# Two pairs of experts per visit, an earlier first block of weights, and stores by halves in a fused GRU and mixture-of-experts kernel

## The chip, the cores and the metric

The kernel runs on one core of a Trainium2 chip. The metric is the device time of one execution in microseconds; for the kernel before it is 2645.92 us, the median of three runs (2645.7 to 2645.97). A core has a matrix engine (TensorE, PE in the profile), three engines for elementwise work (VectorE or DVE, ScalarE or ACT, GpSimd or POOL) and a queue engine (SyncE or SP). DMAs are issued here from SP and POOL. Each engine works through its own list of instructions in order, and semaphores tie the lists together.

## The reference

Two blocks follow each other on x of shape (128, 64, 512), float32: 128 batch rows, 64 time steps, 512 channels. Cut to what matters:

```python
# block 0: a GRU over time, its states through a ternary-weight matrix, added to x
x = x + ffn0(gru(cond, x, W_ih, W_hh, b_ih, b_hh), weight, bias)
# block 1: a causal convolution over 64 steps, and on it a mixture of experts
h = causal_conv(x, taps=cond[:, None, :]) + b
logits = h @ gate_w.T                       # 64 experts, the best 6 of each token
for each token t, each of its experts e (at most 64 tokens per expert):
    y[t] += p[t, e] * (silu(h[t] @ w_gate[e]) * (h[t] @ w_up[e])) @ w_down[e]
shared = silu(h @ sw_gate) * (h @ sw_up) @ sw_down
out = x + y + shared
```

The sizes are H = 512 channels, I = 352 inner channels for an expert and 704 for the shared one; w_gate, w_up and w_down hold 64 experts.

## The kernel before, in words

**The GRU stage** (to about 1400 us in the profile) runs its 64 steps; it is not touched. It leaves x after block 0 in DRAM, in `out` and, by channels, in `x1c`.

**The convolution stage** (1400 to 1466 us) goes through 16 slabs of 32 channels, each against a Toeplitz matrix built from cond (`conv_group`, L182). Buffers `tz0` to `tz3` and `xc0` to `xc3` serve the slabs in turn. L713 adds the bias and writes the result to `hids`, one tile for the first 32 time steps and one for the last 32; L725 adds the products with the two oldest taps, held in `xl`. A time step t has 128 batch rows. `store_first` writes the first four time steps to the table `tab` in DRAM from POOL; the experts later gather their rows there. The last slab's 32 channels of these rows are copied to a tile of their own, `copy`, and stored from it.

**Turning and routing.** `turn` transposes a time step's rows on PE (L1108), and L1118 copies the turned rows back over the same place in `hid`, which must wait until the stores out of that place have landed. `route` makes the logits (`lg`, L1132), the softmax and the six best experts. NB = 4 time steps make an iteration i; there are NI = 16.

**The shared expert** (`shared(i)`) is a generator with 44 pieces per iteration (`PIECES`), and the order in which it is advanced is the order of PE's work. It multiplies in a Winograd form (Strassen's seven products, `winograd`, L809) on blocks of 128 inner channels; `prepare_shared(c)` makes the sums of weights for block c on DVE (`st1`, `st2`, `st4`), and overwrites part of the weights. The weights `swg` and `swu` come by one DMA each, after the gate weights `gw` and the remainder `swr`. In the last iteration the results are added to what stands in `out` (`sums`), and the rows are stored whole from SP (L1079). The earlier iterations add their rows to `out` by accumulating DMAs from POOL (`add_shared`, L1086).

**The experts.** After iteration 8, pairs of experts are woven into the pieces of `shared`. Two experts of 64 slots each share the 128 rows of a pair, each on 64 columns of PE. A pair q goes through four steps: `inputs` transposes the gathered rows (L1478), `gate_up` makes the two products (`pg`, `pu`, L1498) and the gated values `a`, `turn` transposes `a` (L1513), `down` multiplies by w_down (`py`, L1524), copies to `ys` (L1533) and scatters with accumulation to `out` from POOL (L1535). `experts()` is a generator of EPIECES = 97 pieces, which the main loop spreads over the pieces of `shared`:

```python
            while due < EPIECES and due * PIECES * SPREAD < slot * 4 * EPIECES:
                next(routed)
                due += 1
```

So between two pieces of the experts lie two or three of the shared expert. Four sets of buffers (`wexs`) hold the weights of two pairs, loaded from SP by `load_gate_up` and `load_down` as soon as PE has read what they replace. The rows of iterations 8 to 15 wait in DRAM (`xts`) and are loaded by `load_xrows` into two buffers in turn (L1271), on the same SP queue. The gathers (L1455) and scatters stand on POOL's queue. The tile framework gives the order on each engine from the order of the program and an estimate of its own; `tc.issue_after` puts an instruction behind a named one.

Of the kernel before, what the change touches and what calls it, by code (L numbers as in the profile page):

```python
# [8 lines left out]
F32 = mybir.dt.float32  # L9
# [10 lines left out]
P = 128  # L20
B = 128
T = 64
D = 512
# [9 lines left out]
DS = 16  # L33
# [9 lines left out]
def adaln_ffn_kernel(  # L43
# [641 lines left out]
        nc.vector.tensor_add(xl[:, 1], xl[:, 1], tap[:, 1])  # L685


    copy = conv.enter_context(tc.tile_pool(name="copy", bufs=1)).tile([P, 4, 2 * DS], F32, name="copy")

    def store_first(d, rows=None):  # L690
        for t in range(4):
# [5 lines left out]
    with tc.tile_pool(name="ps_c", bufs=4, space=PSUM) as ps_c:  # L697
        for sl in range(NSL):

            if sl >= NCB:  # L700
                load_piece(sl)
            if sl == NSL - 1:

                store_first(slice(0, 2 * DS * (NSL - 2)))
                store_first(slice(2 * DS * (NSL - 2), 2 * DS * (NSL - 1)))
            for g in range(DS // 4):
                if early:
                    ps = early.pop(0)
                else:
                    ps = conv_group(sl, g, ps_c.tile([P, D], F32, name="psc"))  # L710
                d = slice(g * 4, g * 4 + 4)
                for th in range(2):
                    nc.vector.tensor_tensor(  # L713
                        hids[th][:, :, 2 * DS * sl : 2 * DS * (sl + 1)].rearrange(
                            "p t (h d) -> p t h d", h=2
                        )[:, :, :, d],
                        ps[:, :, :, th * TH : (th + 1) * TH].rearrange("p j h t -> p t h j"),
                        cb_h[:, sl, :, d].unsqueeze(1).to_broadcast([P, TH, 2, 4]),
                        ALU.add,
                    )  # L720
            if sl >= NCB:
                if sl == NCB:
                    tail_products()
                d = slice(0 if sl == NCB else 2 * DS * sl, 2 * DS * (sl + 1))
                nc.vector.tensor_add(  # L725
                    hids[1][:, TH - TAIL :, d], hids[1][:, TH - TAIL :, d], xl[:, :, d]
                )
            if sl == NSL - 1:
                nc.scalar.copy(copy, hids[0][:, :4, D - 2 * DS :])
                store_first(slice(D - 2 * DS, D), copy)  # L730
    conv.close()
    gis_.close()

# [15 lines left out]
    st4 = w1.tile([P, HK, full * P], F32, name="st4")  # L749
    st2 = w1.tile([P, HK, full * P], F32, name="st2")  # L750
    st1 = w1.tile([P, HK, full * P], F32, name="st1")
    gw = w1.tile([P, KD, NE], F32, name="gw")
    load_rows(gw, gateT)

    swr = w1.tile([P, KD, 2, rest], F32, name="swr")
    load_rows(swr[:, :, 0, :], sw_gate[:, full * P :])
    load_rows(swr[:, :, 1, :], sw_up[:, full * P :])
    swg = w1.tile([P, KD, full * P], F32, name="swg")
    load_rows(swg, sw_gate[:, : full * P])
    swu = w1.tile([P, KD, full * P], F32, name="swu")  # L760
    loaded = load_rows(swu, sw_up[:, : full * P])

    swdr = w1.tile([P, D], F32, name="swdr")

    sws = {1: swg[:, :HK], 2: swg[:, HK:], 3: swu[:, HK:], 4: st4, 5: st1, 6: st2, 7: swu[:, :HK]}

    def prepare_shared(c):

        w11, w12, w21, w22, t4, t1, t2 = (
            w[:, :, c * P : (c + 1) * P]  # L770
            for w in (sws[1], sws[7], sws[2], sws[3], st4, st1, st2)
        )
        nc.vector.tensor_sub(t1, w12, w11)
# [48 lines left out]
    class Block:  # L822
# [5 lines left out]
        def product(self, n):  # L828
            ps = winograd(
                n,  # L830
                self.accs,
                lambda k: sws[n][:, k, self.c * P : (self.c + 1) * P],
                lambda k: self.ops[n][:, k],
            )
            one, two = self.aT[:, :QT], self.aT[:, QT:]
            if n == 1:
                self.u2 = shu.tile([P, QT], F32, name="u2")
                nc.scalar.copy(self.u2, ps)
            elif n == 6:
                add(self.u2, self.u2, ps)  # L840
            elif n == 7:
                self.u3 = sh.tile([P, QT], F32, name="u3")
                self.summed = add(self.u3, ps, self.u2)
            elif n == 5:
                add(two, ps, self.u3)
                mul(two, two, self.g2)
            elif n == 2:
                self.g1 = sh.tile([P, QT], F32, name="g1")
                nc.scalar.activation(self.g1, ps, AF.Silu)
            elif n == 4:  # L850
                self.g2 = sh.tile([P, QT], F32, name="g2")
                add(self.g2, ps, self.u2)
                nc.scalar.activation(self.g2, self.g2, AF.Silu)
            elif n == 3:
                add(one, ps, self.u2)
                mul(one, one, self.g1)
# [20 lines left out]
    class Down:  # L877
# [54 lines left out]
        def finish(self, rows, sums):  # L932
# [12 lines left out]
            for name, more in (("x", None), ("v", self.v), ("z", self.u2), ("w", self.u2)):  # L945
                j, half_ = self.places[name]
                cols = slice(half_ * HD, (half_ + 1) * HD)
                dst = rows[:, 2 * self.p + j, cols]
                if sums is not None:
                    old = sums[:, 2 * self.p + j, cols]  # L950
                    if more is not None:
                        add(old, old, more)
                    add(old, self.accs[name], old)
                elif more is None:
                    nc.scalar.copy(dst, self.accs[name])
                else:
                    add(dst, self.accs[name], more)
# [9 lines left out]
    def shared(i, sums=None):  # L967
# [44 lines left out]
        for c in range(full):  # L1012
            cur = Block(c, ops, aT)
            for n in (1, 6, 7, 3, 2, 4, 5):
# [6 lines left out]
                if n == 7 and c == 0:  # L1021

                    with tc.issue_after(cur.summed.ins):
                        rest_values()
                if n == 7 and i == 0 and c + 1 < full:
                    prepare_shared(c + 1)
            prev = cur
        if i >= PLAIN:
            after = Down(0, aT, aTr, space)
# [27 lines left out]
        else:  # L1057
            for p in range(2):
# [15 lines left out]
                for name in ("x", "w", "z"):  # L1074
                    down.block(name)
                down.finish(rows_of(i), sums)
                if sums is not None:
                    for t in range(i * NB + 2 * p, i * NB + 2 * p + 2):
                        nc.sync.dma_start(out=out_t[t], in_=sums[:, t % NB])  # L1079
                yield  # L1080
# [175 lines left out]


    slots = ctx.enter_context(tc.tile_pool(name="slots", bufs=1, reuse_waits="tile"))
    xrp = []

    def row_buffer(side):
        xrp.append(
# [4 lines left out]

    def load_xrows(i):
        if i < NI:
            xrows[i] = xrp[i % 2].tile([P, NB, D], F32, name="xr")  # L1270
            nc.sync.dma_start(  # L1271
                out=xrows[i], in_=xts[i * NB - TH : (i + 1) * NB - TH].rearrange("t p d -> p t d")
            )

    row_buffer("left")
    load_xrows(NI // 2)
# [17 lines left out]
    def load_gate_up(q):  # L1294

        if q < NE // 2:
            for e in (2 * q, 2 * q + 1):
                wg = wexs[e % 4].tile([P, KD, EI], F32, name="wg")
                load_rows(wg, w_gate[e])
                wu = wexs[e % 4].tile([P, KD, EI], F32, name="wu")  # L1300
                load_rows(wu, w_up[e])
                weights[e] = [wg, wu]

    def load_down(q):
        if q < NE // 2:
            for e in (2 * q, 2 * q + 1):
                wd = wexs[e % 4].tile([P, len(ech), D], F32, name="wd")
                load_rows(wd[:, :efull, :], w_down[e, : efull * P, :])
                nc.sync.dma_start(out=wd[:n_last, efull, :], in_=w_down[e, efull * P :, :])
                weights[e].append(wd)  # L1310

    weights = {}
    for q in range(2):
# [152 lines left out]
    class Pair:  # L1466
# [5 lines left out]
        def inputs(self):  # L1472
            q = self.q
            rows = gathered.pop(q)
            self.ws = [weights.pop(2 * q + j) for j in range(2)]
# [13 lines left out]
        def gate_up(self):  # L1489
# [5 lines left out]
            for which, acc in ((0, pg), (1, pu)):  # L1495
                for k in range(KD):
                    for j in range(2):
# [4 lines left out]
                            start=(k == 0),  # L1502
                            stop=(k == KD - 1),
                        )
            self.a = a = ex.tile([P, EI], F32, name="a")
# [12 lines left out]
        def down(self):  # L1518
# [50 lines left out]
    for i in range(NI // 2 + 1, NI):  # L1569
        n = i - NI // 2 - 1  # L1570
        sums = None
        if i == NI - 1:

            sums = xrp[(i + 1) % 2].tile([P, NB, D], F32, name="xr")
# [60 lines left out]
```

## Time and profile before

| | us |
|---|---|
| median of three runs | 2645.92 |
| the profiled execution | 2645.99 |
| its span, first to last instruction | 2644.3 |
| PE busy | 2632.3 |
| DVE busy | 1405.0 |
| ACT busy, POOL busy | 427.4, 453.0 |
| convolution stage | about 1400 to 1466 |
| first L1498, last L1524 | 2013.6, 2564.9 |
| last matmul's end | 2639.6 |

The granted clock of TensorE was 1.000 of full speed over the span. Busy times of different engines overlap, so only the longest chain counts. A row such as "PE y L809 <- DVE u L843" says that PE's work on tile y, line 809, waited for DVE's work on u. PE's matmuls are pipelined: the listed length of one is longer than the step to the next, so starts are compared with starts.

### The profile page before, as it was taken

What the parts mean: (1) busy time and instruction counts of PE and PEld (TensorE: products, weight loads), DVE (VectorE), ACT (ScalarE), POOL (GpSimd) and SP (SyncE); (2) the same over time, 40 slices, a digit from 0 to 9 for tenths busy, and PEclk for the clock granted to TensorE, in tenths of its full rate; (3) what the DMA queues carried; (4) which work ended last, traced back from release to release, by engine and by line L of the source; (5) the groups of instructions that cost most, each with busy time, mean ns of one, the idle gap of its engine ahead of it and who ended that gap; (6) DMA issues with size and microseconds to landing.
All of it is one profiled execution on the core that took longest, in us unless ns stands there. A gap on an engine that the chain in (4) does not pass through costs nothing.

```text
span 2644.3 us, 31163 instructions
## 1 busy us (share of the span) xinstructions
PE 2632.3 (100%) x11993; PEld 1825.1 (69%) x11993; DVE 1405.0 (53%) x3110; ACT 427.4 (16%) x794; POOL 453.0 (17%) x516
## 2 busy tenths in 40 slices
PE   9999999999999999999999999999999999999999
PEld 7666666666666666666668767788886666666667
DVE  6555555555555555555557755566674433433344
ACT  1111111111111111111110222222321111111111
POOL 2112111111111111111114100000002222222210
PEclk9999999999999999999999999999999999999999
DMA  5333233232322222322228911222356899998962
GB/s 197 75 58 66 56 60 60 54 61 53 61 47 52 44 52 44 76 44 52 44 58 297 334 37 28 39 66 64 85 145 188 281 315 285 293 332 260 295 182 48
DMA packets 476277, 323.34 MB, mean 122 GB/s; under 512 B 329056, under 2 KB 396512, under 8 KB 473952
## 3 DMA queue, kind: packets, MB, share of 16 engines
q1 hardware_dynamic: 447536, 248.18, 33.6%
q0 software_dynamic: 28592, 73.16, 11.5%
q8 instruction: 95, 1.56, 0.2%
q14 instruction: 54, 0.44, 0.0%
HBM read 235.01 MB, written 92.55 MB: 124 GB/s over the span
## 4 chain that ended last, share of the span: by engine, by line
PE 99%; DVE 0%; DMA 0%; issue 0%; ACT 0%; DVEq 0%
PE psgh L598 25%; PE psz L809 7%; PE psw L809 7%; PE psx L809 7%; PE psz L399 6%; PE psw L399 6%; PE psx L399 6%; PE psf L494 4%; PE y L809 4%; PE py L1524 3%; PE psy L399 3%; PE pg L1498 3%; PE pu L1498 3%; PE y L984 2%; PE psc L182 2%; PE lg L1132 1%
## 5 line engine op out<-in xcount | busy, mean ns | idle before, releaser
L598 PE MATMUL psgh<-whh,hT 128*128 128x512 f32 x1528 | 671.0, 595 | 0.5 <-ACT hT L471 0.5
L598 PEld LDWEIGHTS psgh<-whh,hT 128*128 128x128 f32 x1528 | 285.2, 190 | 348.5 <-issue 334.6
L399 PE MATMUL psx<-wih,xp 128*128 128x256 f32 x744 | 191.0, 379 | 0.0
L220 POOL DMA_DIRECT2D xn<-in_x_dram x61 | 33.9, 555 | 842.2 <-DVE x L506 829.6
L399 PEld LDWEIGHTS psx<-wih,xp 128*128 128x128 f32 x744 | 139.0, 190 | 18.0 <-issue 0.5
L1507 DVE SCALAR_TENSOR_TENSOR a<-a,rw,pu 128x352 f32<-128x352 f32 x32 | 18.6, 580 | 220.4 <-PE pu L1498 220.4
L625 DVE TENSOR_TENSOR n<-psgh,bhn 128x512 f32<-128x512 f32 (+1 forms) x65 | 44.3, 683 | 171.3 <-PE psgh L598 171.3
L471 ACT COPY hT<-psf 128x512 f32<-128x512 f32 x63 | 36.9, 586 | 556.7 <-PE psf L463 556.7
L609 DVE TENSOR_TENSOR r<-psgh,gi 128x512 f32<-128x512 f32 x64 | 44.3, 692 | 139.3 <-PE psgh L598 139.3
L1086 POOL DMA_DIRECT2D out_dram<-hid x32 | 27.6, 1000 | 450.6 <-issue 332.9
L490 POOL TENSOR_TENSOR xn<-xn,fb 128x512 f32<-128x512 f32 x61 | 77.1, 1263 | 143.8 <-DMA xn<-in_x_dram 143.8
L399 PE MATMUL psz<-wih,xs 128*128 128x256 f32 x372 | 95.6, 379 | 0.1
L399 PE MATMUL psy<-t,xs 128*128 128x256 f32 x372 | 95.5, 379 | 0.0
L399 PE MATMUL psw<-t,xp 128*128 128x256 f32 x372 | 95.5, 379 | 0.0
L399 PE MATMUL psz<-t,xs 128*128 128x256 f32 x372 | 95.5, 379 | 0.0
L399 PE MATMUL psw<-wih,xp 128*128 128x256 f32 x372 | 95.4, 379 | 0.0
L494 PE MATMUL psf<-sgn,hhi 128*128 128x512 f32 x256 | 95.0, 492 | 0.3 <-DVE hlo L479 0.3
L1524 PE MATMUL py<-wd,aeT 128*64 128x512 f32 (+1 forms) x384 | 89.5, 601 | 0.0
L628 ACT ACTIVATE n<-n 128x512 f32<-128x512 f32 (+1 forms) x65 | 40.4, 623 | 276.8 <-DVE n L627 276.8
L414 DVE TENSOR_TENSOR p<-psx,bi 128x512 f32<-128x512 f32 x93 | 64.3, 691 | 37.2 <-PE psx L399 37.2
L809 PE MATMUL psx<-xr,swg 128*128 128x256 f32 x320 | 83.3, 383 | 0.0
L809 PE MATMUL psx<-hid,swg 128*128 128x256 f32 x320 | 82.4, 380 | 0.0
(332 smaller groups left out, 4757.4 us busy)
## 6 DMA issues: line engine op xcount, KB each, us to landing
wg<-in_w_gate_dram SPq DMA_DIRECT2D x64, 704.0 KB
wu<-in_w_up_dram SPq DMA_DIRECT2D x64, 704.0 KB
wd<-in_w_down_dram SPq DMA_DIRECT2D x64, 512.0 KB
x1c<-x SPq DMA_DIRECT2D x62, 256.0 KB
out_dram<-x SPq DMA_DIRECT2D x62, 256.0 KB
xn<-in_x_dram POOLq DMA_DIRECT2D x61, 256.0 KB, 4.1
xp<-in_xT_dram POOLq DMA_DIRECT2D x30, 512.0 KB, 5.6
xc<-x1c SPq DMA_DIRECT2D x28, 512.0 KB
```

The source lines that it names most:

```text
L182: i = nc.tensor.matmul(ps[rows, j].rearrange("p h (u t) -> p h u t", u=2), xcs[sl % NCB][:, rows, g * 4 + j], tzs[sl % NCB][:, :, :, g * 4 ...
L399: i = nc.tensor.matmul(ps, self.ops[n][:, k, :], self.ws[n][:, k, :], start=(first and k == 0), stop=(k == HK - 1), skip_group_check=not f ...
L414: add(self.p1, both, b)
L490: nc.gpsimd.tensor_add(xn, xn, fb)
L494: nc.tensor.matmul(ps, piece[:, k, :], sgn[:, k, :], start=(i == 0 and k == 0), stop=(i == 1 and k == KD - 1),)
L598: nc.tensor.matmul(ps[:, piece], hT[:, k, :], whh[c][:, k, piece], start=(k == 0), stop=(k == KD - 1),)
L609: i = nc.vector.tensor_add(r, ps_r, gis.pop((t, 0)))
L625: nc.vector.tensor_add(n[:, p], ps_n[:, p], bhn[:, p])
L809: i = nc.tensor.matmul(ps.rearrange("p (j b) -> p j b", b=P) if len(r.shape) == 3 else ps, lhs(k), r, start=(first and k == 0), stop=(k == ...
L984: nc.tensor.matmul(gu.rearrange("p (j b) -> p j b", b=P), swr[:, k].rearrange("p w n -> p (w n)"), rows[:, k], start=(k == 0), stop=(k == ...
L1498: nc.tensor.matmul(acc[halves[j]], self.xeT[:, k, halves[j]], self.ws[j][which][:, k, :], start=(k == 0), stop=(k == KD - 1),)
L1524: nc.tensor.matmul(py[halves[j]], self.aeT[:n, c, halves[j]], self.ws[j][2][:n, c, :], start=(c == 0), stop=(c == len(ech) - 1),)
```

## The change

Five things are edited. `experts()` handles two pairs in one visit: down, gate_up, down, gate_up follow each other in one piece, and there are 81 pieces instead of 97; `load_gate_up` stands in `gate_up` instead of `turn`, and `ys` has a pool of four buffers instead of two. The rows of iterations 9 to 15 have a third buffer, and their load stands behind the newest load of w_up on SP's queue. The shared expert's weights are split: the first block of 128 inner channels of each has its own tile and is loaded ahead of the other four, and `prepare_shared` of the next block stands behind L843 of this one in iteration 0. The first four time steps' last 64 channels (two slabs instead of one) are copied to a part of `xl` that has been read, and stored from there. And in the last iteration the second two time steps are stored by halves of 256 channels, each right after its sum.

```diff
-    copy = conv.enter_context(tc.tile_pool(name="copy", bufs=1)).tile([P, 4, 2 * DS], F32, name="copy")
+    copy = xl[:, 0, : 16 * DS].rearrange("p (t d) -> p t d", t=4)
...
             if sl == NSL - 1:
-                store_first(slice(0, 2 * DS * (NSL - 2)))
-                store_first(slice(2 * DS * (NSL - 2), 2 * DS * (NSL - 1)))
+                store_first(slice(0, D - 4 * DS))
...
-            if sl == NSL - 1:
-                nc.scalar.copy(copy, hids[0][:, :4, D - 2 * DS :])
-                store_first(slice(D - 2 * DS, D), copy)
+            for n in range(2):
+                if sl == NSL - 2 + n:
+                    d = slice(2 * DS * sl, 2 * DS * (sl + 1))
+                    nc.scalar.copy(copy[:, :, n * 2 * DS : (n + 1) * 2 * DS], hids[0][:, :4, d])
+        store_first(slice(D - 4 * DS, D), copy)
...
+    swg, swu = [None, None], [None, None]
+    others = slice(P, full * P)
+    for which, sw in enumerate((swg, swu)):
+        sw[1] = w1.tile([P, KD, (full - 1) * P], F32, name=f"sw{which}")
     gw = w1.tile([P, KD, NE], F32, name="gw")
...
-    swg = w1.tile([P, KD, full * P], F32, name="swg")
-    load_rows(swg, sw_gate[:, : full * P])
-    swu = w1.tile([P, KD, full * P], F32, name="swu")
-    loaded = load_rows(swu, sw_up[:, : full * P])
+    for which, sw, src in ((0, swg, sw_gate), (1, swu, sw_up)):
+        sw[0] = w1.tile([P, KD, P], F32, name=f"sw{which}first")
+        load_rows(sw[0], src[:, :P])
+    for sw, src in ((swg, sw_gate), (swu, sw_up)):
+        loaded = load_rows(sw[1], src[:, others])
...
-    sws = {1: swg[:, :HK], 2: swg[:, HK:], 3: swu[:, HK:], 4: st4, 5: st1, 6: st2, 7: swu[:, :HK]}
+    sums_ = {4: st4, 5: st1, 6: st2}
+    blocks = {1: (swg, 0), 2: (swg, 1), 3: (swu, 1), 7: (swu, 0)}
+
+    def weights_of(n, c):
+        if n in sums_:
+            return sums_[n][:, :, c * P : (c + 1) * P]
+        sw, h_ = blocks[n]
+        at = max(c - 1, 0) * P
+        return sw[min(c, 1)][:, h_ * HK : (h_ + 1) * HK, at : at + P]
...
                     add(old, self.accs[name], old)
+                    if self.p == 1:
+                        nc.sync.dma_start(out=out_t[(NI - 1) * NB + 2 + j, :, cols], in_=old)
...
+                if n == 7 and i == 0 and c == 0:
+                    marks.append(cur.summed)
                 if n == 7 and i == 0 and c + 1 < full:
-                    prepare_shared(c + 1)
+                    with tc.issue_after(cur.summed.ins):
+                        prepare_shared(c + 1)
...
-                if sums is not None:
+                if sums is not None and p == 0:
                     for t in range(i * NB + 2 * p, i * NB + 2 * p + 2):
                         nc.sync.dma_start(out=out_t[t], in_=sums[:, t % NB])
...
-            xrows[i] = xrp[i % 2].tile([P, NB, D], F32, name="xr")
-            nc.sync.dma_start(
+            xrows[i] = xrp[(i - NI // 2) % 3].tile([P, NB, D], F32, name="xr")
+            with behind(queued):
+                nc.sync.dma_start(
...
-                load_rows(wu, w_up[e])
+                queued.append(load_rows(wu, w_up[e]))
...
     add_shared(NI // 2)
+    row_buffer("left")
     load_xrows(NI // 2 + 2)
...
+    ysp = ctx.enter_context(tc.tile_pool(name="ys", bufs=4, reuse_waits="tile"))
...
# in Pair.gate_up, after the matmuls:
+            load_gate_up(self.q + 2)
# in Pair.turn:
-            load_gate_up(self.q + 2)
# in Pair.down:
-            ys = ex.tile([P, D], F32, name="ys")
+            ys = ysp.tile([P, D], F32, name="ys")
...
-    EPIECES = 3 * NPAIR + 1
+    EPIECES = 5 * NPAIR // 2 + 1
 
     def experts():
         pairs = [Pair(q) for q in range(NPAIR)]
-        pairs[0].inputs()
+        for pair in pairs[:2]:
+            pair.inputs()
+            yield
+        for pair in pairs[:2]:
+            pair.gate_up()
         yield
-        pairs[0].gate_up()
-        yield
-        for q, pair in enumerate(pairs):
-            pair.turn()
-            yield
-            if q + 1 < NPAIR:
-                pairs[q + 1].inputs()
+        for q in range(0, NPAIR, 2):
+            for pair in pairs[q : q + 2]:
+                pair.turn()
                 yield
-            pair.down()
-            if q + 1 < NPAIR:
-                pairs[q + 1].gate_up()
+            for pair in pairs[q + 2 : q + 4]:
+                pair.inputs()
+                yield
+            for pair in pairs[q : q + 2]:
+                pair.down()
+                if pair.q + 2 < NPAIR:
+                    pairs[pair.q + 2].gate_up()
             yield
```

`weights[e]` becomes a dictionary of the three weights of expert e; its uses follow, and `sums` takes its buffer by the new count.

More of the change, by code (lines that the diff above doesn't have):

```diff
@@ L757, in adaln_ffn_kernel @@
     load_rows(swr[:, :, 1, :], sw_up[:, full * P :])
-    swg = w1.tile([P, KD, full * P], F32, name="swg")
-    load_rows(swg, sw_gate[:, : full * P])
-    swu = w1.tile([P, KD, full * P], F32, name="swu")
-    loaded = load_rows(swu, sw_up[:, : full * P])
-    swdr = w1.tile([P, D], F32, name="swdr")
-    sws = {1: swg[:, :HK], 2: swg[:, HK:], 3: swu[:, HK:], 4: st4, 5: st1, 6: st2, 7: swu[:, :HK]}
+    for which, sw, src in ((0, swg, sw_gate), (1, swu, sw_up)):
[3 more added lines that the diff above has]
+        loaded = load_rows(sw[1], src[:, others])
+    swdr = w1.tile([P, D], F32, name="swdr")
+    sums_ = {4: st4, 5: st1, 6: st2}
[6 more added lines that the diff above has]
+        return sw[min(c, 1)][:, h_ * HK : (h_ + 1) * HK, at : at + P]
     def prepare_shared(c):
[L769 to L772, printed above, removed]
+        w11, w12, w21, w22, t4, t1, t2 = (weights_of(n, c) for n in (1, 7, 2, 3, 4, 5, 6))
         nc.vector.tensor_sub(t1, w12, w11)
@@ L831, in product @@
                 self.accs,
-                lambda k: sws[n][:, k, self.c * P : (self.c + 1) * P],
+                lambda k: weights_of(n, self.c)[:, k],
                 lambda k: self.ops[n][:, k],
@@ L1258, in adaln_ffn_kernel @@
     slots = ctx.enter_context(tc.tile_pool(name="slots", bufs=1, reuse_waits="tile"))
-    xrp = []
+    xrp, queued = [], []
     def row_buffer(side):
@@ L1269, in load_xrows @@
         if i < NI:
-            xrows[i] = xrp[i % 2].tile([P, NB, D], F32, name="xr")
-            nc.sync.dma_start(
-                out=xrows[i], in_=xts[i * NB - TH : (i + 1) * NB - TH].rearrange("t p d -> p t d")
-            )
+            xrows[i] = xrp[(i - NI // 2) % 3].tile([P, NB, D], F32, name="xr")
+            with behind(queued):
+                nc.sync.dma_start(
+                    out=xrows[i],
+                    in_=xts[i * NB - TH : (i + 1) * NB - TH].rearrange("t p d -> p t d"),
+                )
     row_buffer("left")
@@ L1300, in load_gate_up @@
                 wu = wexs[e % 4].tile([P, KD, EI], F32, name="wu")
-                load_rows(wu, w_up[e])
-                weights[e] = [wg, wu]
+                queued.append(load_rows(wu, w_up[e]))
+                weights.setdefault(e, {}).update({0: wg, 1: wu})
     def load_down(q):
@@ L1309, in load_down @@
                 nc.sync.dma_start(out=wd[:n_last, efull, :], in_=w_down[e, efull * P :, :])
-                weights[e].append(wd)
+                weights.setdefault(e, {})[2] = wd
     weights = {}
@@ L1474, in inputs @@
             rows = gathered.pop(q)
-            self.ws = [weights.pop(2 * q + j) for j in range(2)]
+            self.ws = [weights[2 * q + j] for j in range(2)]
             ps = ps_e.tile([P, D], F32, name="py").rearrange("p (k b) -> p k b", k=KD)
@@ L1504, in gate_up @@
                         )
+            load_gate_up(q + 2)
             self.a = a = ex.tile([P, EI], F32, name="a")
@@ L1572, in adaln_ffn_kernel @@
         if i == NI - 1:
-            sums = xrp[(i + 1) % 2].tile([P, NB, D], F32, name="xr")
+            sums = xrp[(i + 1 - NI // 2) % 3].tile([P, NB, D], F32, name="xr")
             nc.sync.dma_start(
```

## The prediction

> **What bounds the kernel now.** I read the busy rows and the chain of the page first. TensorE (PE) is the whole span, on the single chain that ended last:
>
> ```profile
> PE 2632.3 (100%) x11993; PEld 1825.1 (69%) x11993; DVE 1405.0 (53%) x3110; ACT 427.4 (16%) x794; POOL 453.0 (17%) x516
> ...
> PE 99%; DVE 0%; DMA 0%; issue 0%; ACT 0%; DVEq 0%
> ```
>
> So only two things can pay: PE's idle time (span 2644.3 less 2632.3 busy, 12.0 us), and time in which PE counts as busy without working at its rate. The windows of ten microseconds put it at 1.1 us at the start, 0.5 before 1400, 5.7 between 1400 and 1500, and 4.7 after the last matmul. The list of who waited for whom names what this change can touch (PE of 1460 to 1500, DVE of 1464 to 1480, SP of 1800 to 2600; microseconds in all, times, the longest):
>
> ```profile
> PE pst L1108 <- DVE hid L1118: 1.3, 1, 1.3
> PE pst L1108 <- DVE hid L713: 1.0, 1, 1.0
> PE psw L809 <- DVE u L843: 0.8, 1, 0.8
> ```
> ```profile
> DVE hid L1118 <- DMA tab<-hid: 2.4, 1, 2.4
> DVE st L773 <- DMA swu<-in_sw_up_dram: 2.0, 1, 2.0
> ```
> ```profile
> SPq L101 <- PE py L1524: 167.0, 25, 15.9
> SPq L1271 <- DMA out_dram<-xr: 135.0, 9, 43.3
> ```
>
> Behind the 1.3 us stands a DMA: L1118 writes the turned rows back over hid, and the stores of hid's channels 448 to 479, issued at 1462.63, landed only at 1468.80. In the expert stage (2013 to 2565) no PE wait is listed. The other kind of loss shows in the timeline of PE across one visit to the experts (start, length, instruction):
>
> ```profile
> 2219.73 1.03 PE L809 MATMUL y<-es,st 128*128 128x256 f32 x4
> 2220.68 2.80 PE L1524 MATMUL py<-wd,aeT 128*64 128x512 f32 x12
> 2223.31 2.54 PE L1498 MATMUL pg<-wg,xeT 128*64 128x352 f32 x16
> 2225.68 2.54 PE L1498 MATMUL pu<-wu,xeT 128*64 128x352 f32 x16
> 2228.14 1.13 PE L809 MATMUL psw<-xr,swu 128*128 128x256 f32 x4
> 2229.11 1.03 PE L809 MATMUL psz<-es,swu 128*128 128x256 f32 x4
> ```
>
> Look at starts, not lengths. Four L809 matmuls take 0.86 us elsewhere. Here the last group before the visit takes 0.95, the first after it 0.97. From start to start of single matmuls in the trace: the step from L809 to L1524 is 0.309 us where 0.216 is usual (+0.093), L1524's first pair takes 0.480 for 0.429 (+0.051), the step out of L1498 0.396 for 0.296 (+0.100), the first L809 matmul afterwards 0.320 for 0.216 (+0.104). One visit costs **0.348 us** in all, with PE counted busy throughout.
>
> [...]The experts' matmuls use 64 columns, the shared ones 128[...]. [...]The last 256 KB store was issued at 2640.76, its last packet ended at 2642.69 and SP passed its last wait at 2643.4[...].
>
> **Part 1, two pairs per visit.** Before: one visit for gate_up(0), 31 for down(q) with gate_up(q+1), one for down(31), 33 in all. In the changed program's order on PE there are 18: one for gate_up of pairs 0 and 1, fifteen of down, gate_up, down, gate_up without another instruction between, and the last two downs, which a shared product separates. Fifteen visits fewer: 15 x 0.348 = **5.2 us**. Matmuls and transposes are the same in number. Inside a visit py is written twice, but L1533's copy (0.585 us) has gate_up's 4.7 us to finish in; pg and pu have a down (2.6 us) between them, their readers take 0.46 and 0.58. These hide.
>
> The four ys buffers remove ACT's wait for a scatter, at most 2.2 us in the trace and never passed on to PE: 0. The third row buffer removes SP's 135.0 us of waiting in front of weight loads. Adding up the bytes that SP issued against those that its queue moved, weights land at least 9 us ahead of use already now, so this is also worth 0. The new order frees weights in bunches. In dense stretches the queue takes 14.3 us for a pair's 4.33 MB (303 GB/s); four loads freed 2.6 to 14.7 us into a visit then land by about 32 us, and the last is needed 40 us after the visit began: 8 us of slack cover it. If the cover goes, each late load is PE's. Moving load_gate_up from turn to gate_up moves four SP issues (0.4 to 0.5 us each) a few microseconds earlier; they wait for the same matmuls.
>
> **Part 2, the first rows.** Channels 448 to 511 now come from the place in xl, by two ACT copies (0.3 us each at most; ACT is idle for 60 us there). POOL issues 8 stores instead of 12 (0.54 us each). L1118 then waits for the stores issued at 1458.50 to 1460.65; at the same 6.2 us they land by 1466.8, and the transposes end at about 1467.1, so the DMA wait is off the path. Then t4 starts behind the four transposes at 1468.3 instead of 1469.74, and L1132's matmuls, which wait for four L1118 copies, at 1469.7 instead of 1471.5: **1.8 us** earlier. The sc tile shares addresses with the new copy as it did with the old, and is first needed at 1476, after those stores (1475).
>
> **Part 3, first block of weights first.** gw, swr and the two first blocks lie where xc0 lay, which is free one slab earlier, so SP issues them near 1453.5 instead of 1457.5 and by an estimate (0.9 MB at some 340 GB/s behind what is queued) they land by 1463, for use at 1469.6; DVE's 2.0 us wait at L773 goes. The rest (2 MB) lands no later than now. Putting prepare_shared(c+1) behind L843 lets L843 run at once: the **0.95 us** PE delay at 1480.4 (0.79 listed) goes. What is late next: on DVE the four subtractions for block 2 (1.35 us) now stand ahead of L855 of block 0, for which PE's psz waits. Stepping PE, DVE and ACT through the new order with the durations of the trace gives PE waits of 0.3 + 0.5 + 0.1 us near 1485 to 1487. Parts 2 and 3: 1.8 + 0.95 - 0.9 = about **1.9 us**, bounds 0.5 and 2.8.
>
> **Part 4, last rows by halves.** Before, SP issued two 256 KB stores at 2640.34 and 2640.76, after the fourth L953 (2640.65). Now one of 128 KB follows each of the four L953 from 2639.65 on, some 0.4 us apart, so the last issue ends at 2641.3 rather than 2641.15, but has only 128 KB behind it. 512 KB took 1.5 us from 2641.18; now the last packet should end near 2642.2 rather than 2642.69: **0.4 us**, bounds -0.1 (SP's issue binds) and 0.7.
>
> **Sum.** 5.2 + 1.9 + 0.4 = 7.5 us off the profiled execution's 2645.99 (span 2644.3 and 1.7 around it): 2638.5. The median of the runs is 2645.92, the same within 0.1.
>
> **Rivals.** (a) The early gains are eaten: DVE is 98% busy in 1480 to 1490, and its new order makes PE wait as long as before. Also, a switch inside a longer visit might not be saved in full. For it: that busy share; against: DVE stands idle 2.4 + 2.0 us just before. Then 5.2 x 0.8 + 0.4 + 0.5: 2640.9.
> (b) Slower: POOL's chain of scatters becomes the bound. Each scatter waits for the one before it, 7.4 us apart at L1535 (179.8 us over 30 waits, and 1.4 of issue). A visit now queues four, behind two gathers: 29.6 us, and the stores of L1086 add 10 us an iteration, 3.5 a visit: 33.1 against some 33.3 between visits. A gather is issued about 28 us of lag before PE's transposes need it. It decides from about 7.9 us a scatter, where fifteen visits use up the 28 us; at 8.4, each of the last eight visits would wait 3.8 us, 30 us in all: about 2668. For it: single scatters took up to 8.9 us; against: the mean, and four ys buffers that let the chain run without gaps.
> (c) Weights late: with the queue at 265 GB/s instead of 303 the 8 us are gone, and dense stretches cost some 10 us: 2648. For it: DMA share 1.00 from 2100 to 2200; against: SP no longer stands still for xr.
> (d) The split visits don't appear as ordered: excluded by the order on PE.
>
> **How the numbers follow.** A measurement of this kernel can tell about 0.2% (5.3 us) from no change. My forecast 0.74, (a) 0.14, (b) 0.07, (c) 0.05. The forecast's own range is 2636.5 to 2640.5. The 80% range goes from 2636.0 to 2643.0, into (a) and a mild (c). Faster by more than 0.2% is below 2640.6: 0.75; within 0.2%: 0.13; slower: 0.12.
>
> **What would show it.** Right: 18 visits, PE's matmuls after and before them unchanged at 0.95 and 0.97; no L1118 wait for tab<-hid; the lg matmuls near 1469.7; SP's wait at the xr load gone; four L953 stores. Wrong: PE waits on wg, wu, wd or rows between 2010 and 2560 (b, c), or on L843, L845 or L855 of more than 1 us near 1485 (a).

## The result and the profile after

The changed kernel takes 2639.58 us (median of 12 runs, 2638.0 to 2641.09) against 2646.07 us (12 runs, 2645.22 to 2647.76) for the kernel before on the same chip: 6.5 us less, a ratio of 0.9974 with a 95% interval of 0.9966 to 0.9982. The forecast was 2638.5, so one microsecond of the expected gain did not come; 2639.58 lies inside the forecast's range. The profiled execution took 2639.73 us for a span of 2637.7. In the changed kernel L1108, L1118, L1132, L984, L809, L843, L1498, L1524 and L953 have become L1127, L1137, L1151, L1000, L823, L857, L1523, L1549 and L967.

Busy rows and chain of the page of the changed kernel:

```profile
PE 2626.6 (100%) x11993; PEld 1826.7 (69%) x11993; DVE 1403.7 (53%) x3110; ACT 427.7 (16%) x795; POOL 451.4 (17%) x512
...
PE 99%; DMA 1%; DVE 0%; issue 0%; POOL 0%; ACT 0%; SPq 0%; DVEq 0%
```

PE still is the whole chain. The span fell by 6.6 us, and PE's busy time by 5.7 of them with the same 11993 matmuls: most of the gain was time in which PE had counted as busy. PE's idle time fell only from 12.0 to 11.1 us.

PE's timeline across one visit to the experts (start, length, instruction; the first line is cut by the window):

```profile
2185.64 1.06 PE L1523 MATMUL pg<-wg,xeT 128*64 128x352 f32 x6
2186.52 2.54 PE L1523 MATMUL pu<-wu,xeT 128*64 128x352 f32 x16
2188.89 2.75 PE L1549 MATMUL py<-wd,aeT 128*64 128x512 f32 x12
2191.47 2.54 PE L1523 MATMUL pg<-wg,xeT 128*64 128x352 f32 x16
2193.84 2.54 PE L1523 MATMUL pu<-wu,xeT 128*64 128x352 f32 x16
2196.30 1.13 PE L823 MATMUL psw<-swd,aT 128*128 128x256 f32 x4
2197.27 1.03 PE L823 MATMUL psz<-space,es 128*128 128x256 f32 x4
```

The second down starts 2.37 us after pu, at the usual pace, without the step of 0.309 us that used to stand in front of a down. Behind the visit L823 takes 0.97 us as before. There are 18 visits, and the boundary itself has not become cheaper: by the same four steps as before, a visit costs 0.348 us in this trace too.

Who waited for whom (PE of 1460 to 1500, then, after the mark, PE of 1500 to 1600; microseconds in all, times, the longest):

```profile
PE pst L1127 <- DVE hid L713: 0.9, 1, 0.9
PE psw L823 <- DVE u L857: 0.3, 1, 0.3
PE y L823 <- DVE st L788: 0.2, 1, 0.2
...
PE psw L823 <- DVE u L857: 0.4, 1, 0.4
```

The waits of 1.3 us (L1108) and 0.8 us (L809) are gone, and three small ones are new. As gaps, that is, by how much a step from start to start exceeds the usual one, they are 0.44 us at 1485.0, 0.36 at 1486.4 and 0.59 at 1541.2; the gaps that went were 1.46 and 0.96. No PE wait is listed in the expert stage. On DVE no wait for tab<-hid or swu is left, and SP's waits at the row load (now L1292) fell from 135.0 to about 13 us.

### The profile page after: what moved, and what is told of

It is laid out like the page before. It is cut to its first block, busy times and chain, and to the rows that moved or that the text cites. A ratio compares the mean times of both kernels' runs of the same rounds, so it can differ in the third digit from the quotient of the medians.

```text
span 2637.7 us, 31178 instructions
## 1 busy us (share of the span) xinstructions
PE 2626.6 (100%) x11993; PEld 1826.7 (69%) x11993; DVE 1403.7 (53%) x3110; ACT 427.7 (16%) x795; POOL 451.4 (17%) x512
## 4 chain that ended last, share of the span: by engine, by line
PE 99%; DMA 1%; DVE 0%; issue 0%; POOL 0%; ACT 0%; SPq 0%; DVEq 0%
PE psgh L598 25%; PE psw L823 7%; PE psz L823 7%; PE psx L823 7%; PE psz L399 6%; PE psw L399 6%; PE psx L399 6%; PE psf L494 4%; PE y L823 4%; PE py L1549 3%; PE psy L399 3%; PE pg L1523 3%; PE pu L1523 3%; PE y L1000 2%; PE psc L182 1%; PE lg L1151 1%
## 5 line engine op out<-in xcount | busy, mean ns | idle before, releaser
L1105 POOL DMA_DIRECT2D out_dram<-hid x32 | 27.6, 1010 | 449.8 <-issue 332.9
L1549 PE MATMUL py<-wd,aeT 128*64 128x512 f32 (+1 forms) x384 | 88.8, 597 | 0.0
L1523 PE MATMUL pg<-wg,xeT 128*64 128x352 f32 x512 | 81.2, 459 | 0.0
L1523 PE MATMUL pu<-wu,xeT 128*64 128x352 f32 x512 | 81.2, 459 | 0.0
```

The costliest lines, as they stand in the source:

```text
L1523: nc.tensor.matmul(acc[halves[j]], self.xeT[:, k, halves[j]], self.ws[j][which][:, k, :], start=(k == 0), stop=(k == KD - 1),)
L1549: nc.tensor.matmul(py[halves[j]], self.aeT[:n, c, halves[j]], self.ws[j][2][:n, c, :], start=(c == 0), stop=(c == len(ech) - 1),)
```

## The experiments

The runs came in three groups of four, each beside runs of the kernel before: its median was 2646.20 us in the first group (parts 1 and 4), 2645.41 in the second (`part_2_only`, `part_3_only`, `old_buffers`, `held_back`) and 2646.31 in the third. Differences from the kernel before are taken within a group; the changed kernel's own is 6.5 us, and a variant is compared with the changed kernel by these two differences. In the variants a line number can lie a few lines beside that of the changed kernel.

**Part 1 alone, part 1 taken out, and a dose.** In `two_pairs_only` the order of the visits and the buffers of the changed kernel are put into the kernel before. `one_pair_again` is the changed kernel with the old `experts()` (EPIECES = 97). `split_67` is the changed kernel with more places to stop at:

```diff
             for pair in pairs[q : q + 2]:
                 pair.down()
+                yield
                 if pair.q + 2 < NPAIR:
                     pairs[pair.q + 2].gate_up()
-            yield
+                    yield
```

> The kernel before with part 1 alone: two pairs of experts per visit, four ys buffers, the third row buffer and the earlier load_gate_up; 18 visits on TensorE instead of 33. Theory (each visit costs 0.348 us of change of tiling, and nothing else in part 1 counts): 15 x 0.348 = 5.2 us less than the kernel before, about 2640.8. Rival (part of it is lost again in the longer visits, or in weights and scatters that come in bunches): 4 us less or fewer, 2642 or more, with waits of PE on wg, wu, wd or rows between 2010 and 2565 in the trace.

Measured: 2640.94 us (17 runs), 5.3 less than the kernel before, ratio 0.9979 (0.9972 to 0.9986); no PE wait in the expert stage.

> The changed kernel with only the order of the visits put back: one pair per visit, 33 visits; the four ys buffers, the third row buffer and parts 2 to 4 stay. Theory: the 15 visits come back at 0.348 us each, 5.2 us more than the changed kernel's 2639.6, about 2644.8; what is left below the kernel before, about 1.3 us, is parts 2, 3 and 4. Rival (the buffers carry a good part of the gain): less than 3 us more, below 2642.6.

Measured: 2645.01 us (13 runs), 5.3 more than the changed kernel; against the kernel before the ratio is 0.9995 (0.9987 to 1.0003). So parts 2 to 4 together give about 1.2 us, where the prediction had 2.3. The interval, from 3.4 us less to 0.8 more, does not exclude 2.3. The 5.3 of `two_pairs_only` and this 1.2 add up to the 6.5 of the whole change.

> The changed kernel with every down and every gate_up in a place of its own among the shared products: 67 visits on TensorE instead of 18, the same matmuls otherwise. Theory (0.348 us for each visit, whatever stands in it): 49 x 0.348 = 17.1 us more than the changed kernel's 2639.6, about 2656.7, with PE counted busy throughout and its listed idle time unchanged. Rival (the price hangs on the pairing of down with gate_up, or on what a visit waits for, not on the change of tiling): well off that line, less than 10 us more, or PE waits in the trace of 2010 to 2565.

Measured: 2658.67 us (5 runs), 19.0 us more than the changed kernel, where 17.1 was expected; no PE wait in the expert stage, and PE's idle time is 10.3 us (11.1 in the changed kernel). The start-to-start gaps between 2000 and 2600 us grew by 16.5 us, 0.337 for each of the 49 visits, so the line holds. The rest is something else. Two downs and one gate_up were cut in the middle (PE's timeline of `split_67`):

```profile
2077.77 1.07 PE L1549 MATMUL py<-wd,aeT 128*64 128x512 f32 x2
2078.77 1.13 PE L823 MATMUL psz<-es,sw 128*128 128x256 f32 x4
2079.83 2.79 PE L1549 MATMUL py<-wd,aeT 128*64 128x512 f32 x10
2082.55 1.13 PE L823 MATMUL y<-space,es 128*128 128x256 f32 x4
```

The cut parts two matmuls of one expert from those of the other expert of the pair. In a whole down of the changed kernel the two of a pair start 0.007 us apart, and the next two 0.43 us behind them. Here the two pieces take 1.003 and 2.721 us from start to start, a whole down 2.728. If each parted matmul takes a step of its own, three such cuts cost an estimated 2.3 us by the usual steps (four times 0.42, twice 0.29), and 16.5 + 2.3 comes within 0.1 of the 18.7 us by which the span grew.

That the price goes with the number of columns (128 to 64 and back, the change of tiling of the expectations) and not with the experts can be read in the changed kernel's trace. Behind the routing product L1151, which also uses 64 columns, the step to L823 is 0.316 us where 0.216 is usual, and the first step of L823 is 0.320 for 0.216: the same +0.100 and +0.104 as behind a visit. Between L1549 and L1523, both of 64 columns, the 30 steps are the usual 0.428 us. What PE does in the longer steps, no trace here shows.

**Which buffer carries part 1.** `old_buffers` is the changed kernel with `bufs=2` for ys, two row buffers in turn and no order between row load and weights; `ys_two` and `rows_two` undo one of the two:

```diff
-            xrows[i] = xrp[(i - NI // 2) % 3].tile([P, NB, D], F32, name="xr")
-            with behind(queued):
+            xrows[i] = xrp[(i - NI // 2) % 2].tile([P, NB, D], F32, name="xr")
+            with nullcontext():
```

> The changed kernel with two pairs per visit, but with two ys buffers and two row buffers as before, and the row load not ordered behind the weights. Theory: SP's long waits at the row load come back (some 100 us in all) and ACT or POOL wait for a scatter now and then, but the weights still land several us ahead of use and PE waits for nothing between 2010 and 2565: 2639.6, no change. Rival (the buffers are what makes bunches of two pairs possible): PE waits on wg, wu, wd or py in that stretch, 5 us or more slower.

Measured: 2644.09 us (13 runs, 2639.89 to 2647.05), only 1.3 less than the kernel before, ratio 0.9995 (0.9986 to 1.0003); the changed kernel has 6.5. My theory fell: with two pairs per visit and the old buffers no more is left than `one_pair_again` has without any longer visit. In its trace PE waited 2.7 us for wg near 2363. Its times spread over 7.2 us, those of the changed kernel over 3.1. All 12 executions of the changed kernel had a granted clock of 1.000; here it was 0.999 in ten (median 2645.0 us) and 1.000 in three (2641.5). The next two runs separate the buffers.

> The changed kernel with two ys buffers instead of four, the third row buffer kept. Theory (in old_buffers it was SP standing 17 us at the row load that made the weights late): ACT waits for a scatter now and then, PE for nothing between 2010 and 2565, 2639.6, no change. Rival (the ys buffers made the loss of old_buffers): 4 us slower, about 2643.5.

Measured: 2640.56 us (14 runs), 5.8 less than the kernel before, ratio 0.9977 (0.9969 to 0.9985). One wait of ACT for a scatter, 9.6 us at 2472, reached PE as a gap of 0.70 us at 2473.0. That is the size of the difference from the changed kernel, and below what the timing can tell.

> The changed kernel with two row buffers instead of three and the row load not ordered behind the weights, the four ys buffers kept. Theory: the loss of old_buffers is all here: SP stands at the row load until a store is done, wd and the loads behind it go out some 9 us late, and PE waits 2 to 5 us on wg, wu or wd in some visit; about 2643.5. Rival (ys): 2639.6.

Measured: 2644.08 us (13 runs, 2640.78 to 2646.86), 2.2 less than the kernel before, ratio 0.9990 (0.9982 to 0.9999): the loss is in the row buffers. The granted clock was 0.999 in seven executions (median 2644.4 us) and 1.000 in six (2642.7). Waits of `rows_two` (PE of 2010 to 2565; SP of 2300 to 2335), then SP's timeline, and behind the mark one line of the changed kernel's:

```profile
PE pg L1522 <- DMA wg<-in_w_gate_dram: 3.0, 1, 3.0
```
```profile
SPq L1292 <- DMA out_dram<-xr: 17.7, 2, 16.5
```
```profile
2311.80 2.15 SPq L101 DMA_DIRECT2D wu<-in_w_up_dram  x1
2331.85 0.37 SPq L1292 DMA_DIRECT2D xr<-xts  x1
2332.31 0.46 SPq L101 DMA_DIRECT2D wd<-in_w_down_dram  x1
...
2324.68 0.37 SPq L101 DMA_DIRECT2D wd<-in_w_down_dram  x1
```

SP stood at the row load until 2331.85, because the buffer still had a store to come that stands behind scatters on POOL. The wd load behind it went out at 2332.31; in the changed kernel, whose times here differ by under 1 us, it went out at 2324.68, as soon as PE had read what it replaces. The run also takes away the row load's place behind w_up, but here the load stands behind the same load of w_up in both kernels, so the buffer made the difference. Of the 7.6 us, 5.6 are left where it counts: the second wg of the next visit landed at 2365.55 instead of 2359.98. PE needs it at about 2362, and waits 3.0 us.

**Parts 2 and 3 one by one.** `part_2_only` and `part_3_only` put these hunks of the diff alone into the kernel before. Each was executed once (2644.72 and 2647.83 us), since a microsecond can't be timed, and is read in its profile.

> The kernel before with part 2 alone: the last 64 channels of the first rows copied to the place in xl, eight stores on POOL instead of twelve. Read in the trace, from the first transposes of the first rows on, since one microsecond can't be timed. Theory (parts 2 and 3 need each other): the wait for tab<-hid goes and the lg matmuls come 1.6 us earlier, 2.8 us after the first transposes instead of 4.4; but swu still lands near 1473.5, so DVE's sums of weights start no earlier, and PE's psw product behind L843 waits for longer than 0.96 us, nearly 2.6: nothing is left of the gain at 1482. Rival (the two parts add): the psw product starts 1.6 us earlier too.

Measured from the first transposes on: lg after 2.74 us (4.41 in the kernel before), the psw product after 14.43 (15.06). Of the 1.66 us that the store's wait gave, 0.63 is left at that product. Waits of `part_2_only` (DVE of 1464 to 1480, PE of 1460 to 1500; L774 and L844 are L773 and L843 of before):

```profile
DVE st L774 <- DMA swu<-in_sw_up_dram: 3.4, 1, 3.4
```
```profile
PE psw L810 <- DVE u L844: 1.6, 1, 1.6
```

DVE waits for swu for 3.4 us instead of 2.0, and PE for L843 for 1.6 instead of 0.8. That is the theory's mechanism at about half its size.

> The kernel before with part 3 alone: first blocks of swg and swu in tiles of their own and loaded first, prepare_shared of the next block put behind the sum of the last (L843). Theory: DVE's 2.0 us wait for swu goes, L1118's 1.3 us wait on PE for the store stays, so lg still comes 4.4 us after the first transposes; the 0.96 us in front of the psw product near 1480 goes, and 0.3 to 0.8 us of new waits stand within the next 7 us: 0.2 to 0.7 us net. Rival (the new order on DVE costs as much as it gives): 0 or a loss.

Measured: the 0.96 us gap is gone, gaps of 0.44 and 0.36 us are new, and the first gap is 1.88 us where it was 1.46, with DVE waiting 2.8 us for tab<-hid instead of 2.4. With another of 0.21 at lg the sum of gaps is 2.89 us against 2.42: 0.5 us worse, outside what was expected. The gaps are not all of the loss. Shortly after PE's waits of 0.95 and 1.72 us the granted clock fell (windows of `part_3_only`; the clock is the third figure from the end):

```profile
1471.00:1472.00 1.00, 1.00 (x6) 0.50 (x6) 1.00 (x3) 0.00 (x0) 0.41 (x1) 0.61 1.07 398
1472.00:1473.00 1.00, 1.00 (x7) 0.98 (x6) 0.97 (x4) 0.00 (x0) 0.00 (x0) 0.50 1.05 388
```

The lg matmuls took 3.9 us from their first start to that of L995, where they take 2.5 in the kernel before: another 1.2 us beside the 0.21. From the first transposes to the first shared product behind the second routing it is 45.0 us, against 43.2 in the kernel before, 42.6 in `part_2_only` and 41.4 in the changed kernel. So alone the parts give 0.6 and -1.8 us (-0.5 by the gaps); together 1.8. With one execution, how often the clock falls there is not known.

**Part 4 undone.**

> The changed kernel with part 4 undone: the last two rows stored whole, by two stores of 256 KB after the fourth final sum instead of four of 128 KB, one after each. Theory: the last packet lands 0.4 to 0.5 us later, and from the last final sum's end to the end of the span it is 3.6 us again instead of 3.1; the median, 2640.0, lies inside what a timing can tell from no change. Rival (SP's issues bind, so nothing changes at the tail): 3.1 us from the last final sum to the end as now.

Measured: 2639.95 us (10 runs), and in the profile 3.5 us from the end of the last final sum to the end of the span, where the changed kernel has 3.1 to 3.2 and the kernel before 3.6. SP's stores of the changed kernel, then of this run:

```profile
2633.58 1.80 SPq L969 DMA_DIRECT2D out_dram<-xr  x4
```
```profile
2634.78 0.81 SPq L1096 DMA_DIRECT2D out_dram<-xr  x2
```

The last final sum ends at 2634.54 and 2635.08, so the last issue ends 0.84 us behind it with four stores and 0.51 with two. The four cost SP 0.3 us, and the tail is shorter all the same. But the last packet ends 1.87 us behind the sum in the changed kernel, 2.06 here and 2.04 in the kernel before: only 0.2 us of the gain are bytes that land earlier. The rest lies between the last packet and the end of the span (1.27, 1.39 and 1.60 us). The step is seen in the profiles only.

**The POOL rival.** `fifth_scatter` adds to each odd pair of the changed kernel a scatter of zeros:

```diff
-            for j in range(2):
+            for n, j in enumerate((0, 1, 0) if q % 2 else (0, 1)):
...
-                    in_=ys[halves[j]],
+                    in_=ys[halves[j]] if n < 2 else zs[:CAP],
```

> The changed kernel with a fifth scatter in every visit: after each odd pair's two scatters a third one adds 64 rows of zeros to the rows of the first. It tests the threshold of the POOL rival. By the prediction's sum a visit then holds 5 x 7.4 us of scatters against some 33 us between visits, 3.7 us too many, 55 us in fifteen visits, of which 28 us of lag are used up first: about 27 us slower than the changed kernel, with PE waiting for rows in the last visits. If POOL has more room than that sum gave it (gathers and stores that are issued inside the scatters' waits): less than 5 us slower.

Measured: 2667.67 us as the median of two runs that lie 12 us apart (2661.52 and 2673.82), 28 us more than the changed kernel. PE of 2010 to 2565 in the profiled one, the faster of the two:

```profile
PE py L1505 <- DMA rows<-tab,idxp: 13.2, 2, 8.5
```

PE waits for gathered rows twice, behind 2353.6 and 2468.2: there the chain of scatters is the bound. In front of the first wait POOL's five scatters start 7.65, 7.62, 5.37 and 7.77 us apart, and the gathers go out behind them, at 2351.94 and 2353.31. With four scatters a visit PE never waits for rows. The size is not the theory's. This execution's span is 21.8 us longer than the changed kernel's. Of that, 13.2 us are these waits, in two visits that are not the last, where the theory had 27 us in the last visits, and some 3 us are slower steps of L823 behind them (the granted clock was 0.50 from 2357 to 2366, around the end of the longer one). Setting the zeros made DVE wait 5.1 us for a store near 1957, and that cost PE another 3.3 us; after it the granted clock was 0.50 from 1962 to 1964.

**Mending what the change brought.** L1023, the last of three sums for rows 8 to 11, stood at 1539.67 in front of L854 and L857 and had waited 1.5 us for a store of `out_dram<-hid`. DVE's line of the changed kernel, then the same sum (L1007) in the kernel before:

```profile
1539.67 0.69 DVE L1023 TENSOR_TENSOR hid<-hid 128x512 f32<-128x512 f32 x1 [1.48 <-DMA out_dram<-hid]
```
```profile
1540.28 0.69 DVE L1007 TENSOR_TENSOR hid<-hid 128x512 f32<-128x512 f32 x1 [1.19 <-DMA out_dram<-hid]
```

`held_back` moves these sums and the selection of the first rows:

```diff
-        with behind(marks if i == 0 else downs):
+        with behind(marks if i == 0 else downs or held):
...
+                if n == 7 and i == 1 and c == 1:
+                    held.append(cur.summed)
...
-                if done * PIECES <= n * 20:
+                if done * PIECES <= n * 20 and (i or done != 3 or n >= 10):
```

> The changed kernel with two moves on DVE. The sums of rows 8 to 11 (L994, L995, L1023), of which L1023 stood in front of L854 and L857 at 1539.67 waiting 1.5 us for a store, come behind the second block of the rows before; the selection of the first rows (L1209 and the two lines after it) comes behind the sums of weights for block 2. Theory: the three waits of PE that the change brought (0.44 at 1485.0, 0.36 at 1486.4, 0.59 at 1541.2) go, 1.2 to 1.4 us less, 2638.3, and no wait in their place over 0.2 us between 1475 and 1600. Rival (a wait moves rather than goes): as much PE idle time in that stretch as now, 2639.6.

Measured: 2638.24 us (7 runs), ratio 0.9972 (0.9960 to 0.9983). The three gaps are gone, and one of 0.58 us stands at 1487.2, behind ACT's L863: both theories have a part.

> The kernel of the run held_back, in which a wait of 0.58 us stood at 1487.2: ACT's L863 had to wait for DVE's L870 to give the buffer g1 free, and L870 came behind the sums of weights for the next block. Here those sums come behind L870 instead of behind L857, for every block but the first. Theory: the last of the new waits goes, PE has no wait over 0.2 us between 1475 and 1600, 0.6 us less than held_back: 2637.7 to 2638 beside a kernel before of 2646. Rival (DVE is full there, so the wait shows at the next link of the chain, the y product behind L788): as much idle time on PE as in held_back, 0.5 us or more.

Measured: 2637.21 us (5 runs, 2636.01 to 2637.69), ratio 0.9965 (0.9951 to 0.9978). All PE waits of 1460 to 1600:

```profile
PE pst L1129 <- DVE hid L713: 0.9, 1, 0.9
```

Only the wait that the kernel before had too is left, and one gap of 0.23 us at 1480.3. By the gaps this version is 1.2 us (1.39 less 0.23) ahead of the changed kernel; its interval overlaps the changed kernel's, and so does that of `held_back`, so the timing alone does not order them.

## Why the prediction was right, and where it was off

**Part 1, 5.2 us: right, and for its reason.** Alone it gave 5.3 us, taken out it cost 5.3, and 67 visits continued the line at 0.337 us a visit. PE waits had no share.

**"The third row buffer ... worth 0", "ys ... 0": these two steps failed.** I priced the row buffer on the order of before, where loads are freed evenly and landed 9 us ahead. In the order of the change the same wait of SP holds up a bunch. The sum came out because the change brings the buffer along, which is luck; without it part 1 is worth about 1 us by the medians: `rows_two` is 2.2 us and `old_buffers` 1.3 us ahead of the kernel before, and parts 2 to 4 alone 1.2. The missing cover could have been read from the trace of before: in the expert stage SP stood 14 to 19 us at the row load, in front of weights, and the prediction gave the dense stretches 8 us of slack. (The wait of 43.3 us ended at 2014.9, when the first visit began.) The 8 us were too many as well. In the changed kernel the second wg of the visit at 2352 lands 38 us after the visit before began, where the prediction had about 32, and only 2.15 us ahead of its first use. The ys buffers were worth 0.7 us in the one trace.

**Parts 2 and 3, 1.9 us: right up to 1490, then a term was missing.** From the first transposes to the psw product behind L857 it is 12.35 us instead of 15.06, 2.71 less, where 1.8 + 0.95 stood in the sum. The new waits took 0.80 of it, where 0.9 stood. By 1490 some 1.8 us were won, and this is sharper than any timing: from the first transposes to the first shared product behind the second routing it is 41.4 us in seven of the eight kernels with both parts and this order on DVE (42.2 in `whole_rows_last`), and 43.2 in both that have neither. The sum then left out 1541: the work on PE came 1.5 us earlier, but the stores of the rows in whose place the sums for rows 8 to 11 are written were issued only 0.76 us earlier (L1105 at 1535.26, L1086 at 1536.02 before), and L1023, which waits for them, ran only 0.61 us earlier on DVE, so PE lost 0.59. `held_back` shows that this was the cause: with L1023 elsewhere in DVE's order the gap is gone. (Its other move, the selection of the first rows, stands some 50 us earlier.) Its place is the step "what is late next", which I followed for one iteration and not for the next.

**Part 4, 0.4 us: the size right, the reason in part.** By the profiles it is 0.3 to 0.5 us. The sum had the last packet 0.4 to 0.5 us earlier; behind the last final sum it came 0.2 us earlier, and the other 0.1 to 0.3 us were saved behind it, for which the sum had no term. The first of the two whole stores of before also did not wait for the fourth sum, as the prediction has it: it went out at 2640.34, and that sum ended at 2640.65.

**The sum.** 5.3 + 1.8 - 0.6 + 0.4 = 6.9 us; the medians differ by 6.5. The rest is not settled: the first transposes came 0.3 us later in the profiled execution than in that of before, and in the runs' profiles they lie anywhere from 1465.7 to 1467.4.

**The rivals.** (a) did not come: no switch was lost in the longer visits. (b) had its threshold in the right place: four scatters a visit leave PE alone, five make it wait. That five cost 28 us where the sum gave 27 is largely chance: the two runs lie 12 us apart, and in the profiled one the waits for rows are 13.2 us. (c) lay nearer than 0.05 suggests: the smallest slack of a weight was 2.15 us and not 8, and what kept the wait away was a part of the change that I had called worthless.

## What to carry to other kernels

When one engine is busy for the whole span, look at the steps between its instructions where their shape changes: grouping work of one shape saved 0.35 us for each visit avoided, that is, for a change from 128 columns to 64 and back, and no busy row shows it. Price a buffer in the order of work that the change makes, not in the present one; a wait that cost nothing between even loads cost some 4 us between bunched ones. And after a gain in one place, follow it into the next iteration, to the first instruction whose store has not become earlier by as much.

## What the runs showed of the hardware that was not expected

A wait of PE can cost more than its length: behind one of 2.7 us in `old_buffers`, steps took about 1.3 us more. Windows of `old_buffers` around its wait for wg, then of `rows_two` (stretch, its length, busy time of PE, PEld, DVE, ACT and POOL with their instructions, granted clock, DMA share, GB/s):

```profile
2350.00:2362.00 12.00, 12.00 (x69) 6.08 (x69) 2.95 (x8) 1.42 (x3) 3.52 (x4) 1.00 1.07 326
2362.00:2366.00 4.00, 1.49 (x8) 0.29 (x4) 0.00 (x0) 0.59 (x1) 1.45 (x1) 0.94 1.05 372
2366.00:2367.00 1.00, 0.78 (x4) 0.43 (x6) 0.00 (x0) 0.00 (x0) 0.00 (x0) 0.50 1.08 379
2368.00:2369.00 1.00, 1.00 (x6) 0.47 (x4) 0.00 (x0) 0.00 (x0) 0.00 (x0) 0.54 1.11 227
```
```profile
2362.00:2366.00 4.00, 1.02 (x8) 0.25 (x7) 0.00 (x0) 0.59 (x1) 1.45 (x1) 1.00 1.06 398
2366.00:2367.00 1.00, 1.00 (x10) 0.52 (x8) 0.00 (x0) 0.00 (x0) 0.00 (x0) 1.00 1.05 383
```

In `old_buffers` the granted clock fell to 0.50 during a wait of 2.7 us, when PE had stood for about 2.0 us; it stayed there for 3.4 us (2365.5 to 2368.9, worked out from the mean clocks above), and after the wait four steps of L1522 took 0.58 to 0.63 us and a fifth 0.45 instead of 0.29, about 1.3 us more in all. In a wait of 3.0 us in `rows_two` it stayed at 1.00. In `part_3_only` it fell to 0.50 after waits of 0.95 and 1.72 us with 1.9 us of transposes between them, some 1.3 us after PE had gone on. In `fifth_scatter`, after a wait of 8.5 us, eight steps of L823 took 0.427 us instead of 0.216, at a granted clock of 0.50.

What set the 2.7 and the 3.0 us apart, no run here shows.

The second surprise is the cut of `split_67`: a whole down of twelve 64-column matmuls, those of the two experts 0.007 us apart, took 2.728 us; with shared products of 128 columns between two of them and the other ten, the two took 1.003 us and the ten still 2.721.
